# Linear attention on a megakernel's fourth layer: the share of EPS in every feature, from products of four rows to transfers and VectorE

## The chip, the core and the metric

The kernel runs on one core of one Trainium2 chip. A core has TensorE for matrix products (PE in the profile, with its weight loads as PEld), VectorE (DVE), ScalarE (ACT), GpSimd (POOL) and SyncE (SP), which issues the transfers. Every engine works through its own list of instructions in order; semaphores order the engines among each other. TensorE writes its results to PSUM, a small memory of eight banks, and the other engines read them there. Everything is in float32.

The metric is device time in microseconds for one launch that computes all four layers for both images of the batch. The kernel before takes 5482.62 us (median of three runs, 5473.6 to 5488.54).

## What is computed

The network has four attention or pooling layers on x of shape (2, 512, 64, 64), each on the group-normalised x and added to it. The change touches the fourth, a linear attention with positive random features (FAVOR), with 8 heads of 64 channels, 4096 tokens per image and m = 256 features:

```python
def _favor_softmax_features(data, proj, is_query):
    data_dash = jnp.einsum('bhnd,md->bhnm', data * normalizer, proj)
    diag = 0.5 * jnp.sum((data * normalizer) ** 2, axis=-1, keepdims=True)
    if is_query:
        stab = jnp.max(data_dash, axis=-1, keepdims=True)
    else:
        stab = jnp.max(data_dash, axis=(-2, -1), keepdims=True)
    return ratio * (jnp.exp(data_dash - diag - stab) + EPS)      # EPS = 1e-4
...
qp = _favor_softmax_features(q, proj, is_query=True)
kp = _favor_softmax_features(k, proj, is_query=False)
context = jnp.einsum('bhnm,bhnd->bhmd', kp, v)
k_sum = jnp.sum(kp, axis=-2)
denom = jnp.einsum('bhnm,bhm->bhn', qp, k_sum)
out = jnp.einsum('bhnm,bhmd->bhnd', qp, context) / denom[..., None]
out = out.transpose(0, 2, 1, 3).reshape(B, N, C) @ Wo
```

A query feature is exp(s - diag - stab) + EPS. Numerator and denominator of the attention may both be multiplied by exp(diag + stab) of their token and head. Then the features are plain exp(s), and EPS becomes one number per token and head, w = EPS * exp(diag + stab), which multiplies the sum of the context over all 256 features (in the numerator) and the sum of k_sum over all features (in the denominator). That is a product of one row of 512 tokens with one row of 64 channels for each head. How this addition is made is what the change is about.

## The kernel before

The kernel treats one image after the other, and the layers in turn. The fourth layer (`layer3`) has two parts. `key_context` goes over the tokens in eight blocks of 512 and gathers `ctxm` (features by heads and channels, with the part that EPS adds for the keys) and `ksum`; its end, `contexts`, overlaps with the first query block's preparation (`Queries.first`). `Queries.run` then goes over the same eight blocks for the queries. P is 128 partitions, TB = 512 tokens, KC = 4 chunks of 128 channels (two heads each), NK = 256 features, NB = 8 blocks.

Two generators make a query block. `Queries.prepare(blk + 1)` makes the queries of the next block: per chunk four products with the weights (through the helper at L133), a copy to `k` with the bias (L1330), squares on GpSimd (L1332), and the score products that serve only to find the largest score per token (L1363), whose maxima VectorE takes from PSUM (L1584). After the fourth chunk it sums the squares (L1341), transposes them (L1347), adds half the norm and the maximum (L1592, `losts`), takes the exponential into `wide` (L1596), in rows 32 c and 32 c + 1 of chunk c, and copies each pair of rows once more into the next chunk's stripe (L1597, L1598), so that four rows lie ready. A transpose (L1602) and a copy (L1604) turn this into `lost_rows`, with tokens along the free dimension.

`Queries.attend(blk)` uses the block that was prepared before. Per chunk it makes the features by products (L1664) and exponentials on ScalarE (L1667), and GpSimd forms `qf_sum`, both halves of the features weighted with `ksum` (L1617, L1619). One chunk later come the sums over features:

- L1631: four products of four rows with 64 columns, `ends` by `lost_rows`. They put the share of EPS into `psD` (denominator) and `psO` (numerator) of both heads. They lie in different stripes of rows and columns of TensorE's array.
- L1635: four products that add the features by `ctxm` to `psO`.
- L1639: two products that add `qf_sum` by `ksum` to `psD`.
- L1642 and L1643: VectorE takes the reciprocal of `psD` and multiplies `psO` with it; the result goes into the place of the queries, `k`.

After four chunks L1648 multiplies with the output weights (four output chunks of four products), L1651 adds the result to x, and L1652 sends it out. The two generators are woven into each other by `in_turn`, and the framework's planner then orders each engine's list by its own estimates, so that an instruction can stand earlier than in the source. `psD` has one PSUM buffer, `psO` two, and the general tile `mm` five.

`ends` is made once per image in `contexts` (L1498 to L1506): two sums over all features by products with ones, 512 wide, then eight small VectorE operations that scale them by 1e-4 and mask them, so that each of the four rows has its own head's values. `row2` is one of the masks, and comes from an input of its own.

Of the kernel before, what the change touches and what calls it, by code (L numbers as in the profile page):

```python
# [8 lines left out]
F32 = mybir.dt.float32  # L9
I32 = mybir.dt.int32  # L10
AF = mybir.ActivationFunctionType
ALU = mybir.AluOpType
# [3 lines left out]
P = 128  # L16
C = 512
KC = C // P
# [914 lines left out]
class Net(General):  # L933
# [353 lines left out]
    def layer3(self, X, Y, d, dst, after_keys):  # L1287

        tc, nc, vec = self.tc, self.nc, self.vec
        with tc.tile_pool(name="l3", bufs=1) as sp:
            proj = sp.tile([P, NK], F32, name="proj")
            nc.sync.dma_start(proj, d["proj"])
            nc.vector.tensor_scalar(proj, proj, HD ** -0.25, None, ALU.mult)

            e2h = sp.tile([P, 32], F32, name="e2h")
            nc.vector.memset(e2h, 0.0)  # L1300
            nc.vector.tensor_scalar(e2h[:, :2], self.e2, 0.5 * HD ** -0.5, None, ALU.mult)
            ctxm = sp.tile([P, 2, NH, HD], F32, name="ctxm")
            ksum = sp.tile([P, 2, NH], F32, name="ksum")

            ends = sp.tile([P, 2, P], F32, name="ends")
            with tc.tile_pool(name="l3b", bufs=2) as wp:
                queries = Queries(self, X, proj, e2h, ctxm, ksum, ends, wp)
                with tc.tile_pool(name="l3a", bufs=1) as kp, \
                        tc.tile_pool(name="l3p", bufs=8, space=PSUM) as pp:
                    row2 = kp.tile([P, P], F32, name="row2")  # L1310
                    nc.sync.dma_start(row2, d["row2"])
                    nmean, rstd, mv = self.group_stats(X, sp, pp, self.mv)
                    self.key_context(X, Y, d, nmean, rstd, mv, row2, queries, kp, wp, pp)
                if after_keys:
                    after_keys()
                with tc.tile_pool(name="l3f", bufs=1) as fp, \
                        tc.tile_pool(name="l3m", bufs=5, space=PSUM) as pp, \
                        tc.tile_pool(name="l3o", bufs=2, space=PSUM) as ppo, \
                        tc.tile_pool(name="l3d", bufs=1, space=PSUM) as ppd:
                    queries.run(dst, fp, pp, ppo, ppd, Y if after_keys else None)  # L1320
        self.ahead.close()
# [42 lines left out]
                                     proj[lo:lo + HD, :], start=True, stop=True)  # L1364
        return pS

    def key_context(self, X, Y, d, nmean, rstd, mv, row2, queries, kp, wp, pp):


        nc = self.nc  # L1370
# [81 lines left out]
        in_turn(prepare(0))  # L1452
        for blk in range(NB - 1):
            in_turn(contract(blk), prepare(blk + 1))
        in_turn(chain(contract(NB - 1), self.contexts(top, acc, asum, vmean, row2, queries, kp, pp)),
                queries.first(nmean, rstd, pp))

    def contexts(self, top, acc, asum, vmean, row2, queries, kp, pp):

        nc, ctxm, ksum = self.nc, queries.ctxm, queries.ksum  # L1460

# [31 lines left out]
            nc.vector.tensor_tensor(ksum[:, j, :], ps[:, :NH], lost, ALU.add)  # L1493
            yield
        ends = queries.ends
        for i, src in enumerate((ctxm, bcast(ksum, 3, HD))):
            ps = pp.tile([P, TB], F32, name="mm")
            for j in range(2):  # L1498
                nc.tensor.matmul(ps, self.one, src[:, j], start=(j == 0),
                                 stop=(j == 1))  # L1500
            for cc in range(KC):
                lo = 32 * cc if i else 32 * ((cc + 1) % KC)
                q = slice(lo, lo + 32)
                mine = self.cst[q, C_ROW:C_ROW + P] if i else row2[q, :]
                nc.vector.scalar_tensor_tensor(ends[q, i, :], ps[q, cc * P:(cc + 1) * P], 1e-4,
                                               mine, ALU.mult, ALU.mult)  # L1506
        yield


# [16 lines left out]
class Queries:  # L1526


    def __init__(self, net, X, proj, e2h, ctxm, ksum, ends, wp):
        self.net, self.nc, self.X, self.proj, self.e2h = net, net.nc, X, proj, e2h  # L1530
        self.ctxm, self.ksum, self.ends, self.wp = ctxm, ksum, ends, wp
        new = lambda shape, name: wp.tile(shape, F32, name=name, bufs=1)
        self.bq = new([P, KC], "bq3")
        self.tops, self.lost = (new([P, N // P, NH], name) for name in ("tops", "losts"))
        self.wide = new([P, NT, P], "wide")
        self.nc.gpsimd.memset(self.wide, 0.0)
        self.made = {}
# [35 lines left out]
    def prepare(self, blk, pp):  # L1573
# [18 lines left out]
        nc.vector.tensor_tensor(src, cols, tops[:, ts].rearrange("p t (c h) -> p t c h", h=2),  # L1592
                                ALU.add)

        w = wide.rearrange("p t (c r) -> p t c r", r=32)
        nc.scalar.activation(w[:, :, :, :2], src, AF.Exp)  # L1596
        nc.scalar.copy(w[:, :, 1:, 2:4], w[:, :, :3, :2])  # L1597
        nc.scalar.copy(w[:, :, 0, 2:4], w[:, :, 3, :2])  # L1598
        yield
        ps = pp.tile([P, TB], F32, name="mm")  # L1600
        for t in range(NT):
            nc.tensor.transpose(ps[:, t * P:(t + 1) * P], wide[:, t, :], net.ident)  # L1602
        rows = self.wp.tile([P, TB], F32, name="lost_rows")
        nc.scalar.copy(rows, ps)  # L1604
        self.made[blk] = qs, rows
        yield

    def attend(self, blk, ratio, dst, fp, pp, ppo, ppd):
        nc, X, ends, ctxm, ksum = self.nc, self.X, self.ends, self.ctxm, self.ksum
        qs, rows = self.made.pop(blk)  # L1610
        made_f, sums = {}, {}
        for i in range(KC + 1):
            if i < KC:
                made_f[i] = f = self.features(qs[:, i], fp, pp)
# [6 lines left out]
            if i:  # L1621
                cc = i - 1
                f = made_f.pop(cc)
                psD = ppd.tile([P, TB], F32, name="psD")
                psO = ppo.tile([P, TB], F32, name="psO")
                heads = [slice(h * HD, (h + 1) * HD) for h in range(2)]
                for ch in heads:
                    for i2, ps in ((1, psD), (0, psO)):

                        lo = 32 * cc if i2 else 32 * ((cc + 1) % KC)  # L1630
                        nc.tensor.matmul(ps[ch, :], ends[lo:lo + 4, i2, ch], rows[lo:lo + 4, :],  # L1631
                                         start=True, stop=False)
                for j in range(2):
                    for h, ch in enumerate(heads):
                        nc.tensor.matmul(psO[ch, :], ctxm[:, j, 2 * cc + h, :], f[h][j],  # L1635
                                         start=False, stop=(j == 1))
                for h, ch in enumerate(heads):
                    g = 2 * cc + h
                    nc.tensor.matmul(psD[ch, :], ksum[:, 0, g:g + 1].to_broadcast([P, HD]),  # L1639
                                     sums[cc][h], start=False, stop=True)  # L1640

                nc.vector.reciprocal(qs[:, cc, :], psD)  # L1642
                nc.vector.tensor_tensor(qs[:, cc, :], psO, qs[:, cc, :], ALU.mult)  # L1643
                yield
        for oc in range(KC):
            ps = pp.tile([P, TB], F32, name="mm")
# [693 lines left out]
def arrays_of(i):  # L2340
# [49 lines left out]
    for q in range(4):  # L2390
        for h in range(2):
# [12 lines left out]
        "taps": taps,  # L2404
        "tok32": np.pad(tok.reshape(P, KC, 2, 9).transpose(0, 1, 3, 2).reshape(P, KC, 18),
                        ((0, 0), (0, 0), (0, 14))),

        "row2": (p[:, None] % 32 == 2 + p[None, :] // HD).astype(f), "bv_row": b_kv[None, C:],
        "pb_rows": np.broadcast_to(a["L0_conv_b_proj"], (P, C)),
        "bproj_row": a["L0_conv_b_proj"][None, :],  # L2410
        "W_q": a["L0_conv_W_q"], "W_kv": a["L0_conv_W_kv"], "W_sr": a["L0_conv_W_sr"],
# [27 lines left out]
```

## Time and profile before

| | before |
|---|---|
| median time | 5482.62 us |
| span of the profiled run | 5487.7 us |
| TensorE (PE) busy | 5220.8 us, 95% |
| VectorE (DVE) busy | 3060.8 us, 56% |
| ScalarE (ACT) busy | 1797.6 us, 33% |
| GpSimd (POOL) busy | 1802.7 us, 33% |
| moved by DMA | 276.37 MB, 50 GB/s over the span |
| mean granted TensorE clock | 0.970 |
| L1631, products of four rows | 512 records, 587 to 741 ns each, median 638 |
| L1642, reciprocal | 64 times 3357 ns |
| L1643, product with the reciprocal | 64 times 687 ns |

The instructions of a line are listed with the engine, the tile written and the tiles read, the shape, the number, and the time of one. TensorE's records overlap, since its products are pipelined and products in different stripes of the array run side by side; what a group costs is read from the start of its first record to the start of the next group. A float32 product shows as two records. The query parts of the fourth layer lie at about 2295 to 2760 us (first image) and 5000 to 5480 us (second image).

### The profile page before, as it was taken

How to read it: one execution, taken by the hardware profiler on the slowest of the kernel's cores; microseconds unless marked ns; L12 is line 12 of the kernel's file. 1: busy time of each engine (PE TensorE's matmuls, PEld its weight loads, DVE VectorE, ACT ScalarE, POOL GpSimd, SP SyncE). 2: the span in 40 equal slices, each digit the busy share in tenths (PEclk: the TensorE clock that was granted, in tenths of full speed). 3: DMA queues.
4: the chain of work that ended last, by engine and by line, in shares of the span. 5: the costliest groups of instructions: out<-in, count | busy, mean ns of one | idle time of the engine just before them, and what ended most of it. 6: DMA issues, size and time to landing. Idle time of an engine off the chain costs nothing. (4 is left out here: it accounts for less than half of the span.)

```text
span 5487.7 us, 51928 instructions
## 1 busy us (share of the span) xinstructions
PE 5220.8 (95%) x19291; PEld 2262.9 (41%) x19291; DVE 3060.8 (56%) x3804; ACT 1797.6 (33%) x3441; POOL 1802.7 (33%) x1198
## 2 busy tenths in 40 slices
PE   7999999999988899999999999999999889999999
PEld 4433333554333444544344333335543334445443
DVE  3256667745679533544432666666456894334444
ACT  1245555233213233212212555542432222332221
POOL 0025555401310145434400355553013001554443
PEclk9999999999989999999999999999999999999999
DMA  3024445500000000200010344454000000000000
GB/s 140 2 66 118 126 125 157 148 18 24 1 2 0 1 1 3 75 21 34 31 53 2 83 126 126 125 150 148 1 24 1 2 0 1 1 8 16 16 16 24
DMA packets 103354, 276.37 MB, mean 50 GB/s; under 512 B 15090, under 2 KB 28146, under 8 KB 101044
## 3 DMA queue, kind: packets, MB, share of 16 engines
q1 hardware_dynamic: 103092, 272.97, 17.0%
q8 instruction: 154, 2.52, 0.2%
q14 instruction: 108, 0.88, 0.1%
HBM read 224.68 MB, written 48.23 MB: 50 GB/s over the span
## 5 line engine op out<-in xcount | busy, mean ns | idle before, releaser
L133 PE MATMUL mm<-big,w 128*128 128x512 f32 x2560 | 1186.4, 608 | 5.2 <-DVE late L2223 5.1
L133 PEld LDWEIGHTS mm<-big,w 128*128 128x128 f32 x2560 | 467.0, 191 | 685.1 <-issue 587.6
L2270 POOL TENSOR_TENSOR late<-late,big 128x1024 f32<-128x1024 f32 x192 | 454.5, 2367 | 302.2 <-DVE big L2266 292.3
L1265 POOL TENSOR_TENSOR total<-prob 128x512 f32<-128x512 f32 x128 | 159.6, 1269 | 759.6 <-ACT prob L1262 759.6
L1617 POOL TENSOR_SCALAR qf_sum<-qf,ksum_ratio 128x512 f32<-128x512 f32 x128 | 198.8, 1562 | 552.5 <-ACT qf L1667 351.6
L1182 PE MATMUL acc<-big,dg 128*128 128x512 f32 x704 | 318.9, 610 | 58.0 <-DVE big L697 27.1
L1438 POOL TENSOR_TENSOR big<-big 128x512 f32<-128x512 f32 x224 | 277.4, 1272 | 237.0 <-ACT big L1429 237.0
L2191 POOL TENSOR_TENSOR late<-late 128x512 f32<-128x512 f32 x128 | 160.6, 1275 | 490.5 <-ACT late L2180 448.3
L1642 DVE RECIPROCAL k<-psD 128x512 f32<-128x512 f32 x64 | 214.8, 3357 | 185.0 <-PE psD L1639 185.0
L697 DVE TENSOR_TENSOR big<-big 128x3968 f32<-128x3968 f32 x72 | 308.8, 4289 | 6.9 <-ACT big L698 0.5
L2266 DVE TENSOR_TENSOR big<-big,mm 128x512 f32<-128x512 f32 x384 | 254.4, 679 | 87.4 <-ACT mm L2263 85.9
L1429 ACT ACTIVATE big<-mm,ed 128x256 f32<-128x256 f32 x512 | 193.8, 489 | 277.8 <-DVE top L1425 250.1
L2263 ACT COPY mm<-big 128x512 f32<-128x512 f32 x384 | 220.5, 594 | 158.1 <-DMA big<-rows 117.8
L1363 PE MATMUL mm<-proj,k 64*128 64x256 f32 x2048 | 266.0, 392 | 0.9 <-ACT k L1330 0.9
L1282 DVE RECIPROCAL recip<-psD 128x512 f32<-128x512 f32 x64 | 214.9, 3357 | 87.2 <-PE psD L1279 87.2
L1262 ACT ACTIVATE prob<-mm 128x512 f32<-128x512 f32 x256 | 132.0, 605 | 364.4 <-PE mm L1259 359.2
L1584 DVE TENSOR_REDUCE tops<-mm 128x2 f32<-128x512 f32 x256 | 159.3, 680 | 163.5 <-PE mm L1363 163.3
L2131 DVE TENSOR_TENSOR prod<-qs,big 128x1024 f32<-128x1024 f32 x192 | 230.4, 1215 | 31.1 <-PE tap L2144 29.1
L2270 POOL TENSOR_TENSOR late<-late,tap 128x1024 f32<-128x1024 f32 x96 | 226.6, 2361 | 62.8 <-DVE tap L2266 44.3
L1363 PEld LDWEIGHTS mm<-proj,k 64*128 64x128 f32 x2048 | 208.1, 188 | 95.1 <-issue 78.7
L133 PE MATMUL mm<-big,big 128*128 128x512 f32 x512 | 239.7, 631 | 0.0
L2144 PE MATMUL tap<-prod,cst 128*32 128x512 f32 x768 | 228.7, 618 | 8.7 <-DVE prod L2131 8.6
(369 smaller groups left out, 8397.4 us busy)
## 6 DMA issues: line engine op xcount, KB each, us to landing
big<-rows SPq DMA_DIRECT2D x384, 256.0 KB, 4.0
tap<-rows SPq DMA_DIRECT2D x192, 256.0 KB, 4.0
yd<-late SPq DMA_DIRECT2D x32, 512.0 KB, 4.0
out<-big SPq DMA_DIRECT2D x64, 256.0 KB, 2.0
big<-in_W_kv SPq DMA_DIRECT2D x8, 1024.0 KB, 6.0
rows<-late SPq DMA_DIRECT2D x64, 128.0 KB, 2.4
big<-yd SPq DMA_DIRECT2D x16, 512.0 KB, 4.5
big<-in_x SPq DMA_DIRECT2D x4, 2048.0 KB, 7.6
```

What stands on the lines that cost most here:

```text
L133: self.nc.tensor.matmul(ps, w[:, kc, :], X[:, kc, blk * TB:(blk + 1) * TB], start=(kc == 0), stop=(kc == KC - 1))
L697: nc.vector.tensor_tensor(o, a, b, ALU.max)
L1182: nc.tensor.matmul(accs[b], dg, src[:, b * TB:(b + 1) * TB], start=(j == 0), stop=(j == 6))
L1282: nc.vector.reciprocal(r, psD)
L1363: nc.tensor.matmul(pS[h][i][:, t, :], k[lo:lo + HD, tok:tok + P], proj[lo:lo + HD, :], start=True, stop=True)
L1438: nc.gpsimd.tensor_tensor(a, a, part, ALU.add)
L1642: nc.vector.reciprocal(qs[:, cc, :], psD)
L2131: self.nc.vector.tensor_tensor(self.prods[k % 3].rearrange("p (y x) -> p y x", x=W), qs, self.kx[:, y + dy:y + dy + self.UY, dx:dx + W], A ...
L2144: nc.tensor.matmul(ps[32 * q:32 * q + 32, :], self.cst[:, C_TAPW + 16 - 2 * k:C_TAPW + 48 - 2 * k], self.prods[k % 3][:, j * TB:(j + 1) * ...
L2263: nc.scalar.copy(ps, part)
L2266: nc.vector.tensor_tensor(part.rearrange("p (y x) -> p y x", x=W), self.vx[:, y:y + self.UY // 2, dx:dx + W], ps.rearrange("p (y x) -> p y ...
L2270: nc.gpsimd.tensor_tensor(out, out, self.taps[k % 3], ALU.add)
```

## The change

The share of EPS no longer goes through TensorE. `prepare` writes the eight rows of `lost_rows` (four chunks, two heads) to a tile in DRAM with two transfers. In `attend`, `fetch` reads a head's row of 512 tokens back onto all 64 channels of that head: two transfers of 64 x 512 per chunk, into the tile `lost_all`, which has one buffer. `ends` becomes a column per chunk and kind, so that VectorE can use it as a value per partition. VectorE adds the share to `psD` in place, takes the reciprocal in place, adds the share to `psO` into `lost_all`, and multiplies the two. The fetch for the next chunk stands after that.

`ends` is now made by 32 products of one column instead of four of 512 columns; the masks, the input `row2` and the two copies of rows in `wide` go. `lost_rows` has one buffer instead of two.

```diff
@@ contexts
-        for i, src in enumerate((ctxm, bcast(ksum, 3, HD))):
-            ps = pp.tile([P, TB], F32, name="mm")
-            for j in range(2):
-                nc.tensor.matmul(ps, self.one, src[:, j], start=(j == 0),
-                                 stop=(j == 1))
-            for cc in range(KC):
...
-                nc.vector.scalar_tensor_tensor(ends[q, i, :], ps[q, cc * P:(cc + 1) * P], 1e-4,
-                                               mine, ALU.mult, ALU.mult)
+        ps = pp.tile([P, TB], F32, name="mm")
+        for i in range(2):
+            for g in range(NH):
+                ch = slice(g % 2 * HD, (g % 2 + 1) * HD)
+                for j in range(2):
+                    src = ksum[:, j, g:g + 1].to_broadcast([P, HD]) if i else ctxm[:, j, g, :]
+                    at = i * KC + g // 2
+                    nc.tensor.matmul(ps[ch, at:at + 1], src, self.one[:, :1], start=(j == 0),
+                                     stop=(j == 1))
+        nc.vector.tensor_scalar(ends, ps[:, :2 * KC].rearrange("p (i c) -> p i c", i=2), 1e-4,
+                                None, ALU.mult)
@@ Queries.prepare
-        nc.scalar.copy(w[:, :, 1:, 2:4], w[:, :, :3, :2])
-        nc.scalar.copy(w[:, :, 0, 2:4], w[:, :, 3, :2])
...
-        rows = self.wp.tile([P, TB], F32, name="lost_rows")
+        rows = self.wp.tile([P, TB], F32, name="lost_rows", bufs=1)
         nc.scalar.copy(rows, ps)
-        self.made[blk] = qs, rows
+        lost = self.yp.tile([2, KC, TB], F32, name="lost")
+        for h in range(2):
+            nc.sync.dma_start(lost[h], rows[h:P:32, :])
+        self.made[blk] = qs, lost
@@ Queries.attend
+        def fetch(cc):
+            ends_of[cc] = t = fp.tile([P, TB], F32, name="lost_all")
+            for h in range(2):
+                nc.sync.dma_start(t[h * HD:(h + 1) * HD, :], bcast(lost[h, cc], 0, HD))
+
+        fetch(0)
...
-                for ch in heads:
-                    for i2, ps in ((1, psD), (0, psO)):
-
-                        lo = 32 * cc if i2 else 32 * ((cc + 1) % KC)
-                        nc.tensor.matmul(ps[ch, :], ends[lo:lo + 4, i2, ch], rows[lo:lo + 4, :],
-                                         start=True, stop=False)
...
-                nc.vector.reciprocal(qs[:, cc, :], psD)
-                nc.vector.tensor_tensor(qs[:, cc, :], psO, qs[:, cc, :], ALU.mult)
+                t = ends_of.pop(cc)
+                nc.vector.scalar_tensor_tensor(psD, t, ends[:, 1, cc:cc + 1], psD, ALU.mult,
+                                               ALU.add)
+                nc.vector.reciprocal(psD, psD)
+                nc.vector.scalar_tensor_tensor(t, t, ends[:, 0, cc:cc + 1], psO, ALU.mult, ALU.add)
+
+                nc.vector.tensor_tensor(qs[:, cc, :], t, psD, ALU.mult)
+                if cc + 1 < KC:
+                    fetch(cc + 1)
```

## The prediction

> **What bounds the kernel now.** First the page, engines and slices:
>
> ```profile
> PE 5220.8 (95%) x19291; PEld 2262.9 (41%) x19291; DVE 3060.8 (56%) x3804; ACT 1797.6 (33%) x3441; POOL 1802.7 (33%) x1198
> ...
> L1642 DVE RECIPROCAL k<-psD 128x512 f32<-128x512 f32 x64 | 214.8, 3357 | 185.0 <-PE psD L1639 185.0
> ```
>
> TensorE is busy 95% of the span, VectorE 56%: time taken off TensorE counts unless a wait takes its place. The fourth layer runs once for each image. In its query part, about 2295 to 2760 and 5000 to 5480 us, one block of 512 tokens takes 61.3 us; the windows of two such blocks, one per image (columns: length, then busy us of PE, PEld, DVE, ACT, POOL, then clock, DMA share, GB/s):
>
> ```profile
> 2400.20:2461.50 61.30, 61.30 (x257) 26.33 (x256) 28.64 (x29) 12.72 (x25) 26.31 (x20) 1.00 0.05 18
> 5113.00:5174.30 61.30, 61.30 (x257) 26.32 (x256) 28.64 (x30) 12.73 (x25) 26.31 (x20) 1.00 0.05 18
> ```
>
> TensorE has no gap, at full clock; DVE and DMA are mostly idle. So TensorE sets the length of a block. Its timeline at the end of a block, start and length in the first two columns:
>
> ```profile
> 2441.94 0.64 PE L1631 MATMUL psD<-lost_rows,ends 4*64 4x512 f32 x1
> ...
> 2442.96 1.94 PE L1635 MATMUL psO<-qf,ctxm 128*64 128x512 f32 x8
> 2444.72 1.03 PE L1639 MATMUL psD<-qf_sum,ksum 128*64 128x512 f32 x4
> 2445.68 3.70 PE L133 MATMUL mm<-big,w 128*128 128x512 f32 x8
> 2449.32 0.64 PE L1631 MATMUL psO<-lost_rows,ends 4*64 4x512 f32 x1
> ...
> 2450.33 1.94 PE L1635 MATMUL psO<-qf,ctxm 128*64 128x512 f32 x8
> 2452.10 1.03 PE L1639 MATMUL psD<-qf_sum,ksum 128*64 128x512 f32 x4
> 2453.06 2.00 PE L1363 MATMUL mm<-proj,k 64*128 64x256 f32 x16
> 2454.99 3.89 PE L1648 MATMUL mm<-k,w 128*128 128x512 f32 x8
> 2458.80 1.07 PE L1341 MATMUL mm<-sq,e2h 128*32 128x512 f32 x8
> 2459.80 0.70 PE L1648 MATMUL mm<-k,w 128*128 128x512 f32 x1
> ```
>
> Read starts against starts. The four products of four rows (L1631) run beside each other and cost 2442.96 - 2441.94 = 1.02 us per channel chunk; all undisturbed ones of the 64 read 1.01 or 1.02. A block has four chunks, G0 to G3, whose L1631 start 11.3, 11.3, 7.4 and 31.3 us apart: the short gap is the one from G2 to G3. VectorE in it:
>
> ```profile
> 2445.83 3.36 DVE L1642 RECIPROCAL k<-psD 128x512 f32<-128x512 f32 x1 [2.45 <-PE psD L1639]
> 2449.22 0.69 DVE L1643 TENSOR_TENSOR k<-psO,k 128x512 f32<-128x512 f32 x1
> 2453.20 3.36 DVE L1642 RECIPROCAL k<-psD 128x512 f32<-128x512 f32 x1 [3.29 <-PE psD L1639]
> 2456.48 0.63 DVE L1584 TENSOR_REDUCE tops<-mm 128x2 f32<-128x512 f32 x1
> 2457.02 0.67 DVE L1643 TENSOR_TENSOR k<-psO,k 128x512 f32<-128x512 f32 x1
> ```
>
> After G3's L1639 ends (2453.06) VectorE needs until 2457.7, and the last L1648 of the first output chunk waits for it. By lengths TensorE needs 1.93 + 3.43 + 0.1 + 1.0 = 6.46 us up to the L1648 of 2459.80 and takes 6.74: 0.28 us of wait.
>
> **What the Trainium skill says.** (1) "TensorEngine Tiling (Array Packing)", Key Properties: a change of tiling mode drains TensorE. The trace agrees: eight L1648 take 3.43 us before products of the same tile shape and 3.53 before another, 0.1 us per switch. (2) "TensorE: Matmul & The Clock Gate", Part 1: The HAM clock gate: an idle window of about 3.4 us halves the clock. In the trace it takes less: an idle stretch of some 1.7 us (4408.9 to 4410.7) left the clock at 1.00, one of 2.7 (3668.5 to 3671.1) was followed by half clock. Windows of 1 us, PE busy is the second number, the clock the third from the right:
>
> ```profile
> 4409.00:4410.00 1.00, 0.00 (x0) 0.00 (x0) 1.00 (x1) 0.38 (x1) 0.00 (x0) 1.00 0.00 0
> ...
> 3670.00:3671.00 1.00, 0.00 (x0) 0.00 (x0) 1.00 (x1) 0.72 (x2) 0.97 (x1) 1.00 1.10 246
> ...
> 3673.00:3674.00 1.00, 1.00 (x3) 0.42 (x2) 1.00 (x2) 0.56 (x1) 0.46 (x1) 0.50 0.26 49
> ```
>
> Such an episode loses 1.7 us, summed over its windows. (3) "DMA: Bandwidth & Descriptors", Anatomy of one DMA, puts the fixed cost of one at about 2.0 us; the trace's smallest loads (64 KB) land after 1.9 to 2.0.
>
> **The change, part by part.** I call D the end of a chunk's L1639 (D2 for G2, D3 for G3).
>
> Removed on TensorE: L1631, 4 x 1.02 = 4.08 us per block. In the built order two of the eight score products (L1363 before) move between psO's and psD's products of G3, which adds two mode switches, 0.2. Net -3.9 us per block.
>
> Added on VectorE, per chunk: two scalar_tensor_tensor; reciprocal and product stay. The nearest rows are L553 (0.75, one PSUM operand) and L1643 (0.69); I take 0.70. The chain becomes 0.15 + 0.70 + 3.36 + 0.70 + 0.69 + 0.1 of hand-overs = D + 5.7 (before D + 4.2). psD has one buffer and is now held to the last of these. G0 to G1 and G1 to G2: the next L1639 starts 9.3 us after D (11.3 - 1.02 - 0.96), so it doesn't wait. G2 to G3: 3.64 (L133) + 1.77 (psO) + 0.5 + 0.1 = D2 + 6.0; GpSimd's sums, which L1639 also needs, are done at D2 + 5.8 already now (2451.49). So 0.3 us to spare. VectorE gets 4 x 1.4 = 5.8 us more per block, 34 of 57: no bound.
>
> Added transfers: two writes and eight reads of 128 KB per block. The first read of a block follows about 7 us after the copy of the rows (2407.1), and its chunk ends at 2423: hidden. The other three wait for the last VectorE operation on the single lost_all buffer, D + 5.7; the second transfer is issued 0.33 us later (the L1652 issue takes 332 ns). Time to land: nearest row is proj, 128 KB from DRAM, 2.5 us; floor 2.0, ceiling 4.0 (the row of 256 KB loads). I take 2.5: data at D + 5.75 + 0.33 + 2.5 + 0.1 = D + 8.7. The next chunk ends at D + 10.3 in the long gaps: hidden by 1.6. In the short one D3 = D2 + 6.95, so VectorE starts at D3 + 1.7. Queued behind it are G3's chain and one score reduction that is put into it, then another: 0.70 + 0.63 + 3.36 + 0.70 + 0.63 + 0.69 + 0.1 = 6.8, so k is ready at D3 + 8.5. In the built order TensorE has, before it needs k: six score products 1.5, three L1648 2.65, L1341 1.0, three L1648 of the next output chunk (these come earlier than before) 2.65, two transposes 0.3: D3 + 8.1. Wait 0.4 against 0.28 now: +0.1. Ends: 0 with a landing of 2.0, 1.9 with one of 4.0.
>
> So -3.8 us per ordinary block. There are seven per image; the first block of the first image is left out, since VectorE is full there (24 BATCH_NORM_STATS2 from 2286 on, G0 to G1 take 12.5): 13 x -3.8 = -49.
>
> ACT's two copies per block (0.2 each) and the row2 load go: off the path, nothing.
>
> Sums for `ends`, once per image: from the first L1499 (2278.88) to L1664 (2286.11) is 7.2 us now. It becomes 32 products of one column, 64 passes. L1491 has such at 128 weight columns: 3.65 us / 32 = 0.114 at full clock, 6.95 / 32 = 0.217 at half. With 64 columns I bound one by half of these and the whole; the clock is at half there (2269 to 2284), so 7 to 14, taken as 9.5 with the 0.9 of L1602: +3, and +1 for a clock that stays low longer. +4 x 2 = +8 (0 to 18).
>
> Last block of an image, no products of a next one: chunk after chunk is VectorE 5.6, transfer 2.8, so 8.4 apart, against 7.8, 7.3, 7.1 now; from G0's D (5.85 after its start, set by GpSimd): 0.15 + 5.6 + 3 x 8.4 = 31 for the last k, then four L1648 left, 3.4 at full clock, 6.9 at half: about 43.5 against 41.3 (5439.09 to 5480.36). +2.5 x 2 = +5 (0 to 12).
>
> Sum: -49 + 8 + 5 = -36: **5447 us**.
>
> **Rivals.** *The transfer takes the place of the products, in part*: landing 4.0. k comes 1.5 later, -2.3 per block, 13 x -2.3 = -30; three fetches each in the last blocks +9; +13 as above: -8, 5475. For it: the 256 KB loads read 4.0. Against: those run beside others, here DMA is 5% busy. *The wait halves the clock*: landing of 5 or so (64 reads of the same 2 KB in DRAM, which no row shows). The wait is then over 2.5 and draws 1.7 of half clock: -3.9 + 2.6 + 1.7 - 0.3 = +0.1 per block, last blocks +13 + 5, sums +8: about +27, **5510**, slower. Against: 0.05 DMA share. *Nothing is given back*: landing 2.0, sums at their floor, last blocks even: 13 x -4.1 = -53, 5430.
>
> **How the numbers follow.** Forecast 0.58, late transfer 0.16, halved clock 0.12, nothing given back 0.14. Faster by over 0.3% (below 5466) are forecast and floor, all but 0.01: 0.71; within: the late transfer, 0.17; slower: 0.12. The range 5424 to 5478 leaves out the halved clock and a little on either side.
>
> **What would show it.** Blocks 57.5 us apart with TensorE full and clock 1.00; lost_all landing in 2.3 to 2.8; VectorE's first operation of G3 waiting for a DMA, of G0 to G2 for psD; L1655 (the old L1648) waiting under 0.5 us for VectorE. Wrong, if the clock column falls to 0.5 once a block, if psD's product waits for VectorE in the short gap, or if the 64 one-column passes take over 14 us.

## The result, and the profile after

The changed kernel takes **5444.11 us** (median of four runs, 5439.77 to 5451.38) beside 5483.76 for the kernel before on the same chip: a ratio of 0.9931, 95% interval 0.9913 to 0.995. On another chip it was 5458.11 beside 5487.34, 0.9949 (0.9935 to 0.9963). It is faster, by a little over half a per cent.

The two pairs differ by ten microseconds, so single effects are not read from the total below but from stages of the profiled run. From the first product of `ends` to the end of an image the changed kernel took 466.5 and 463.3 us (images 0 and 1) on the first chip and 466.0 and 463.6 on the second. The stretch that no edit touches, from the end of image 0's queries to the first product of `ends` in image 1, took 2233.7 and 2251.1. The stages, in us, image 0 and image 1:

| stage | before | after |
|---|---|---|
| first product of `ends` to the end of G0's psD product, first block | 20.3, 20.6 | 20.3, 20.2 |
| from there to the same product of the last block (seven blocks) | 426.8, 425.6 | 406.8, 405.5 |
| from there to the end of the image | 37.6, 36.1 | 39.4, 37.6 |
| sum | 484.7, 482.3 | 466.5, 463.3 |

The sums fall by 18.2 and 19.0, 37.2 together; the span of the profiled run falls by 38.1 (5487.7 to 5449.6). The gain lies in the seven blocks, 20.0 each time; the last block gives back 1.8 and 1.5; the sums for `ends` cost nothing.

The lines of the page that answer to those shown of before (L1655 is the old L1648, the product with the output weights):

```profile
PE 5161.0 (95%) x18891; PEld 2254.2 (41%) x18891; DVE 3144.7 (58%) x3918; ACT 1793.0 (33%) x3409; POOL 1803.2 (33%) x1198
...
L1655 PE MATMUL mm<-k,w 128*128 128x512 f32 x512 | 242.0, 612 | 14.1 <-DVE k L1648 14.1
```

TensorE has 60 us less to do and VectorE 84 more. The second line is new in kind: TensorE now stands 14.1 us in front of this product, all of it until VectorE's last operation of a chunk (L1648) has written `k`: 8.7 us in the fourteen blocks before the last ones, the rest in front of the last products of the two images. The windows of two blocks of image 1 (length, then busy us of PE, PEld, DVE, ACT, POOL, clock, DMA share, GB/s):

```profile
5074.20:5132.10 57.90, 57.69 (x228) 25.43 (x226) 34.20 (x38) 12.45 (x24) 26.37 (x21) 1.00 0.11 37
5132.20:5190.20 58.00, 57.66 (x226) 25.41 (x226) 34.16 (x38) 12.41 (x24) 26.34 (x21) 1.00 0.10 37
```

A block takes 58 us, not 61.3, at full clock; before, PE's first number equalled the length, now 0.2 to 0.3 us are missing. Over the first six blocks of image 1 the mean is 58.3 (349.8 / 6; before 367.8 / 6 = 61.3). Where TensorE stands is in its timeline after G3's psD product (L1640), which ends at 5144.05, D3:

```profile
5142.34 0.70 PE L1362 MATMUL mm<-proj,k 64*128 64x256 f32 x4
5142.97 1.08 PE L1640 MATMUL psD<-qf_sum,ksum 128*64 128x512 f32 x4
...
5149.24 2.84 PE L1655 MATMUL mm<-k,w 128*128 128x512 f32 x6
5151.92 0.38 PE L1346 MATMUL mm<-cst,sq 128*128 128x128 f32 x2
5152.65 1.98 PE L1655 MATMUL mm<-k,w 128*128 128x512 f32 x4 [0.34 <-DVE k L1648]
```

The last product waits 0.34 us for `k`. In the seven blocks of image 1 this wait is 0.2 to 1.4 us, 4.38 together, 0.63 each. VectorE in the same stretch:

```profile
5144.71 1.29 DVE L1583 TENSOR_REDUCE tops<-mm 128x2 f32<-128x512 f32 x2 [2.20 <-PE mm L1362]
5146.20 0.76 DVE L1643 SCALAR_TENSOR_TENSOR psD<-lost_all,ends,psD 128x512 f32<-128x512 f32 x1 [0.20 <-DMA lost_all<-lost]
5146.86 0.69 DVE L1583 TENSOR_REDUCE tops<-mm 128x2 f32<-128x512 f32 x1
...
5151.91 0.68 DVE L1648 TENSOR_TENSOR k<-lost_all,psD 128x512 f32<-128x512 f32 x1
```

G3's first operation starts at D3 + 2.15, released by the transfer, and `k` is there at D3 + 8.54. This is one of the quicker blocks: in all seven of image 1 the fetch is issued at D3 - 1.5, but G3 starts between D3 + 2.0 and D3 + 3.2, and the wait for `k` is long where G3 starts late (0.21 us for a start at 2.02, 1.41 for one at 3.22). In the last block nothing covers the transfer. VectorE there:

```profile
5409.83 0.69 DVE L1648 TENSOR_TENSOR k<-lost_all,psD 128x512 f32<-128x512 f32 x1
5414.12 0.75 DVE L1643 SCALAR_TENSOR_TENSOR psD<-lost_all,ends,psD 128x512 f32<-128x512 f32 x1 [3.61 <-DMA lost_all<-lost]
```

From the end of one chunk's work to the start of the next it waits 3.6 us for the data, and so after each of the first three chunks (3.61, 3.74, 3.58). These two places, the short gap and the last block, are what the experiments take apart.

### The profile page after: what moved, and what is told of

Same layout as the page of the kernel before. It is cut to its first block, busy times and chain, and to the rows that moved or that the text cites. A ratio compares the mean times of both kernels' runs of the same rounds, so it can differ in the third digit from the quotient of the medians.

```text
span 5449.6 us, 51666 instructions
## 1 busy us (share of the span) xinstructions
PE 5161.0 (95%) x18891; PEld 2254.2 (41%) x18891; DVE 3144.7 (58%) x3918; ACT 1793.0 (33%) x3409; POOL 1803.2 (33%) x1198
## 5 line engine op out<-in xcount | busy, mean ns | idle before, releaser
L1362 PE MATMUL mm<-proj,k 64*128 64x256 f32 x2048 | 268.9, 393 | 0.9 <-ACT k L1329 0.9
L1655 PE MATMUL mm<-k,w 128*128 128x512 f32 x512 | 242.0, 612 | 14.1 <-DVE k L1648 14.1
L1583 DVE TENSOR_REDUCE tops<-mm 128x2 f32<-128x512 f32 x256 | 161.5, 684 | 160.2 <-PE mm L1362 159.9
L1362 PEld LDWEIGHTS mm<-proj,k 64*128 64x128 f32 x2048 | 206.5, 188 | 105.7 <-issue 90.1
```

What stands on the lines that cost most here:

```text
L1362: nc.tensor.matmul(pS[h][i][:, t, :], k[lo:lo + HD, tok:tok + P], proj[lo:lo + HD, :], start=True, stop=True)
L1655: nc.tensor.matmul(ps, self.wo[:, kc, oc * P:(oc + 1) * P], qs[:, kc, :], start=(kc == 0), stop=(kc == KC - 1))
```

## The experiments

The theory after the result: **the transfer**. `lost_all` has one buffer, so a fetch starts only when the chunk before is done, and in the short gap and in the last block its data comes late. The rival: **the chain**, four VectorE operations from psD to `k`, is too long wherever the data is. The first four runs set these against each other. Line numbers below are each kernel's own and shift by a few.

**Two buffers.** The fetches stand one chunk further ahead.

```diff
-        rows = self.wp.tile([P, TB], F32, name="lost_rows", bufs=1)
+        rows = sqs[1]
...
-            ends_of[cc] = t = fp.tile([P, TB], F32, name="lost_all")
+            ends_of[cc] = t = fp.tile([P, TB], F32, name="lost_all", bufs=2)
...
         fetch(0)
+        fetch(1)
...
-                if cc + 1 < KC:
-                    fetch(cc + 1)
+                if cc + 2 < KC:
+                    fetch(cc + 2)
```

> The changed kernel with two lost_all buffers, the first two chunks fetched at the start of a block and chunk cc+2 after chunk cc (lost_rows lies in a buffer of sqs, to make room). Transfer theory: what keeps a block at 58.0 us, not 57.3, is that the one lost_all buffer is fetched late, so that in the short gap VectorE starts G3 2.15 us after D3. With two buffers it starts at D3 + 0.15, k is ready near D3 + 6.7 to 7.0 in place of 8.5, the 0.4 to 1.8 us of wait at L1655 go, blocks are 57.3 to 57.6 us apart, and the gaps of 3.6 us between the chunks of the last blocks go (3 x 3 x 2 = 18 us at most, less what GpSimd and TensorE then bound): about 5425 us, 0.989 of before. Chain theory (rival): the four VectorE operations on the way from psD to k are the limit, wherever the data is: blocks stay at 58, last blocks at 41 to 42: 5440 to 5446, 0.993.

Measured: 5437.25 us, 0.990 (0.9885 to 0.9915). The last block is as the transfer theory has it: 31.8 us to the end of the image in both images, in place of 39.4 and 37.6. VectorE there:

```profile
5406.01 0.69 DVE L1649 TENSOR_TENSOR k<-lost_all,psD 128x512 f32<-128x512 f32 x1
5407.97 0.76 DVE L1644 SCALAR_TENSOR_TENSOR psD<-lost_all,ends,psD 128x512 f32<-128x512 f32 x1 [1.27 <-PE psD L1641]
```

The wait of 3.61 for the transfer has become one of 1.27 for psD. The ordinary blocks are a miss: 58.1 us, when 57.3 to 57.6 were expected. VectorE starts G3 at once, and TensorE waits all the same, for something else. First TensorE, then VectorE:

```profile
5146.58 4.56 PE L1656 MATMUL mm<-k,w 128*128 128x512 f32 x10 [0.67 <-DVE tops L1583]
```

```profile
5140.73 0.76 DVE L1644 SCALAR_TENSOR_TENSOR psD<-lost_all,ends,psD 128x512 f32<-128x512 f32 x1 [1.61 <-PE psD L1641]
5141.39 0.69 DVE L1583 TENSOR_REDUCE tops<-mm 128x2 f32<-128x512 f32 x1
5141.99 3.36 DVE L1646 RECIPROCAL psD<-psD 128x512 f32<-128x512 f32 x1
...
5145.85 0.68 DVE L1583 TENSOR_REDUCE tops<-mm 128x2 f32<-128x512 f32 x1
```

G3's scores fill four of the five `mm` buffers, and each comes free when its reduction (L1583) is done. The first output chunk takes the fifth and the squares' sum (L1340) the first that comes free. Early data moved G3's chain ahead of the reductions in VectorE's list: only one stands before the reciprocal, the second runs at 5145.85, and the second output chunk, whose turn comes at 5145.9 with the end of L1340, waits until 5146.58 for that buffer. A wait of 0.63 for `k` was traded for one of 0.67 for `tops`.

**The products left out, nothing in their place.** The share of EPS is missing from the query's numerator and denominator, so this is a bound, not a version.

```diff
-                for ch in heads:
-                    for i2, ps in ((1, psD), (0, psO)):
-
-                        lo = 32 * cc if i2 else 32 * ((cc + 1) % KC)
-                        nc.tensor.matmul(ps[ch, :], ends[lo:lo + 4, i2, ch], rows[lo:lo + 4, :],
-                                         start=True, stop=False)
...
```

> The kernel before without the four products of four rows (L1631) and with nothing in their place: what EPS adds to numerator and denominator is left out of the computation. Products theory: 1.02 us for each of 64 chunks is what the change can win, 65 us; blocks 57.2 us apart (-4.1), the last blocks -2 to -4 each: 5415 to 5425 us, 0.988. Rival, a wait takes their place: without the products TensorE reaches the first L1648 that needs k earlier, VectorE's chain does not move, and G3's k is then the limit: blocks 58 or more, 5435 or more, 0.992, near the changed kernel.

Measured: 5421.11, 0.9874 (0.9857 to 0.9891), within the forecast of the products theory. The query parts are 901.1 us, 65.9 below before, where 64 x 1.02 = 65 was counted. Blocks are 57.7, not 57.2: with the short gap a microsecond shorter, G3's psD product reaches the end of GpSimd's sums. In TensorE's timeline it takes 1.54, not 1.03:

```profile
5122.66 1.54 PE L1633 MATMUL psD<-qf_sum,ksum 128*64 128x512 f32 x4
```

In the changed kernel two score products (four records, L1362 at 5142.34 above) stand in between, and that wait does not show.

**Four transfers in place of two**, the same bytes.

```diff
-                nc.sync.dma_start(t[h * HD:(h + 1) * HD, :], bcast(lost[h, cc], 0, HD))
+                for q in (slice(0, TB // 2), slice(TB // 2, TB)):
+                    nc.sync.dma_start(t[h * HD:(h + 1) * HD, q], bcast(lost[h, cc, q], 0, HD))
```

> The changed kernel with each fetch in four transfers of 64x256 in place of two of 64x512: the same bytes, two more issues on SyncE, 0.48 us each by the trace of the changed kernel, so the data comes about 1 us later. Transfer theory (a fetch after the previous chunk's last VectorE operation is on the path in the short gap and in the last blocks, and nowhere else): +1.0 per block x 14 and +1.0 x 3 in each of two last blocks = +20, about 5464 us, 0.996; more, 5475 to 5490, if the longer wait at L1655 halves the clock. Chain theory (rival): the transfer is hidden, 5440 to 5448.

Measured: 5460.72, 0.9943 (0.9928 to 0.9958), which overlaps with both measurements of the changed kernel. The stages show two effects that cancel. The last block is longer by 3.4 and 4.9 us, where 3 was expected. The ordinary blocks are shorter, 57.8 in place of 58.3, although the data is later: a miss for the transfer theory. VectorE in image 1:

```profile
5150.59 1.89 DVE L1583 TENSOR_REDUCE tops<-mm 128x2 f32<-128x512 f32 x3 [1.89 <-PE mm L1362]
5153.52 0.76 DVE L1644 SCALAR_TENSOR_TENSOR psD<-lost_all,ends,psD 128x512 f32<-128x512 f32 x1 [1.04 <-DMA lost_all<-lost]
```

D3 is 5149.93, so G3 starts at D3 + 3.6. But the planner, which orders by its own estimates, put three reductions ahead of it and TensorE's products with `k` later: all four transposes and one product of the third output chunk now come first. In image 0 that hides the late data altogether. In the fourth block (D3 is 2505.37) G3 starts at D3 + 3.0 and `k` comes at D3 + 9.0, and TensorE runs through without a wait:

```profile
2508.35 0.76 DVE L1644 SCALAR_TENSOR_TENSOR psD<-lost_all,ends,psD 128x512 f32<-128x512 f32 x1 [0.42 <-DMA lost_all<-lost]
...
2513.68 5.32 PE L1656 MATMUL mm<-k,w 128*128 128x512 f32 x12
```

From the second block to the sixth of image 0 the blocks are 57.4 to 57.7 us, and in the changed kernel 57.9 to 59.1. So in the ordinary blocks the order counts as much as the arrival, and TensorE's own order is part of it.

**The numerator first**, with two buffers, so that three operations and not four follow psD.

```diff
+                nc.vector.scalar_tensor_tensor(qs[:, cc, :], t, ends[:, 0, cc:cc + 1], psO, ALU.mult,
+                                               ALU.add)
                 nc.vector.scalar_tensor_tensor(psD, t, ends[:, 1, cc:cc + 1], psD, ALU.mult,
                                                ALU.add)
                 nc.vector.reciprocal(psD, psD)
-                nc.vector.scalar_tensor_tensor(t, t, ends[:, 0, cc:cc + 1], psO, ALU.mult, ALU.add)
-
-                nc.vector.tensor_tensor(qs[:, cc, :], t, psD, ALU.mult)
+                nc.vector.tensor_tensor(qs[:, cc, :], qs[:, cc, :], psD, ALU.mult)
```

> The kernel of two lost_all buffers, and the numerator's addition goes first and into qs, before psD is ready: three operations stay between psD and k (4.9 us by the trace's lengths, not 5.6). Transfer theory: the data was the limit, so after two buffers this brings little more: 1 to 3 us, 5422 to 5424. Chain theory: the length of the chain after D is the limit, so this brings its 0.7 us per block where two buffers alone brought nothing: 14 x 0.7 + 8 x 0.7 = 15, near 5428. Either way blocks are not below 57.2, the length without the products.

Measured: 5448.82, 0.9926 (0.9912 to 0.994). Both theories miss. The chain is shorter (the last blocks take 30.6 and 30.8, 1.0 and 1.2 less than with two buffers), and ordinary blocks are longer, 58.5. The planner put G3's psD product ahead of all scores again, where it takes 1.53, and the products that need `k` early, before the squares' sum. So neither arrival nor length of the chain alone decides an ordinary block.

**A new theory: the order.** After D3 VectorE has about 8 us of work that TensorE waits for: G3's chain, which ends in `k`, and the reductions, which free `mm`. Without waits, TensorE's own work lasts as long. So late data costs (`k` late), and an order with the reductions behind the chain costs as well (`tops` late); as long as TensorE asks for `k` as early as in the changed kernel, one must repair both to gain. Two lines make the other order: a step in the generator, so that the reductions are recorded before G3's reciprocal.

**Two buffers and the reductions first.** Against the kernel with two buffers:

```diff
+                if cc == KC - 1:
+                    yield
                 nc.vector.reciprocal(psD, psD)
```

> The kernel of two lost_all buffers, with one more step of the generator between the first and the second VectorE operation of chunk G3. In the built order two of the score reductions (L1583) then stand ahead of G3's reciprocal, and the other two ahead of k, where in the kernel of two buffers one stands ahead of the reciprocal, one ahead of k and two behind it. Order theory: in the kernel of two buffers the transfer is out of the way, and what is left is that TensorE's second output chunk waits 0.67 us per block for the second reduction, which frees a PSUM buffer of mm, because that reduction stands behind the chain. Freed at D3 + 2.1 here, the wait goes; k comes near D3 + 8.2, and TensorE needs it at D3 + 8.2. Blocks 57.4 to 57.7, not 58.1, last blocks as with two buffers: 14 x 0.5 = 7 us less than that kernel, 5428 to 5432 where it had 5437. Rival (VectorE's list is full after D3, so every order costs TensorE about 0.7): the wait moves to k, blocks stay at 58.0 to 58.2 and the time at 5437.

Measured: 5423.74, 0.9885 (0.9867 to 0.9902), and in a second measurement 5423.93, 0.9882 (0.986 to 0.9904). Blocks are 57.2 us, even less than the 57.4 to 57.7 expected. A window of one:

```profile
5071.20:5128.40 57.20, 57.20 (x228) 25.51 (x226) 34.18 (x38) 12.41 (x23) 26.34 (x20) 1.00 0.11 38
```

PE's time equals the length again. The products of the output weights now run through in TensorE's timeline; D3 is 5127.78, and `k` comes at 5135.65, before the first product that needs it:

```profile
5133.31 4.46 PE L1658 MATMUL mm<-k,w 128*128 128x512 f32 x10
```

The step changed TensorE's list too: the squares' sum (L1340) now stands ahead of all products of the output weights, and the transposes ahead of the second output chunk. What this brings and what the place of the reductions brings is not separated. The order alone, below, has the same order on TensorE in this stretch; it differs from this kernel only by the buffers and the place of `lost_rows`.

The same kernel again:

> The kernel with two buffers and the reductions first once more, beside the other two: blocks 57.2 us apart with no wait of TensorE in them, query parts of 451 us from the first product of ends to the image's end, 0.987 to 0.990 of before.

**The order alone**, with one buffer and the late fetch: the changed kernel plus the same two lines.

> The changed kernel, one lost_all buffer and the late fetch, with the extra step of the generator for G3 alone. In the built order two reductions stand ahead of G3's first VectorE operation, two between it and the reciprocal. Both-theory (in the blocks either thing alone is worth little, since a late chain and a late reduction each cost TensorE about 0.7): the data comes near D3 + 2.0 as in the changed kernel, so k is ready near 2.15 + 0.76 + 1.3 + 3.4 + 0.67 + 0.2 + 0.7 = D3 + 9.1, and TensorE needs it at D3 + 8.2: a wait of 0.8 to 0.9 us, blocks near 58.0, last blocks 37.5 to 39 as in the changed kernel, total 5450 to 5458, 0.994. Order theory alone (the order is the whole loss in the blocks, and the transfer is hidden there): blocks 57.2 to 57.4, last blocks 37.5 to 39: 12 us above the kernel with two buffers and this order, 5436, 0.991.

Measured: 5452.28, 0.9933 (0.9915 to 0.995), blocks 58.3, last block 37.7 in image 1: no better than the changed kernel, as the both-theory says. TensorE in the same place (D3 is 5144.51):

```profile
5153.27 1.98 PE L1657 MATMUL mm<-k,w 128*128 128x512 f32 x4 [0.48 <-DVE k L1650]
```

With the reductions ahead, `k` is late by the transfer. The four cases side by side, with the other kernels below: the mean of the first six blocks of image 1, the wait per block that TensorE's timeline names in the seven blocks of image 1, the last block of image 1, and both query parts together.

| | block | wait per block | last block | query parts |
|---|---|---|---|---|
| changed kernel | 58.3 | 0.63, for k | 37.6 | 929.8 |
| two buffers | 58.1 | 0.67, for tops | 31.8 | 914.4 |
| order alone | 58.3 | 0.79, for k | 37.7 | 930.6 |
| two buffers and order | 57.2 | 0 | 31.8 | 902.3 |
| before | 61.3 | (none named) | 36.1 | 967.0 |
| products left out | 57.7 | for GpSimd, inside psD's product | 29.3 | 901.1 |
| four transfers | 57.8 | 0.2, for k | 42.5 | 930.8 |
| numerator first | 58.5 | 0.67, for k | 30.8 | 916.1 |

In the ordinary blocks either repair alone brings 0.0 to 0.2 us and both together 1.1. In the last block the buffers bring it all. The four transfers show that this pair of repairs is not the only way: with one buffer and later data their blocks are shorter by 0.5 than the changed kernel's, because TensorE asks for `k` later.

**The placing of lost_rows alone**, control of the two buffers.

```diff
-        rows = self.wp.tile([P, TB], F32, name="lost_rows", bufs=1)
+        rows = sqs[1]
```

> The changed kernel with nothing but lost_rows placed in a buffer of sqs: the control of the kernel with two buffers, which needed that room. If the placing costs nothing, it does what the changed kernel does: blocks 57.8 to 58.5, last blocks with 9.1 to 9.3 us from chunk to chunk, 5444. If the placing were the reason of what two buffers brought, its last blocks would be 6 to 7 us shorter.

Measured: 5460.92, 0.9947 (0.9931 to 0.9964); blocks 58.3, last block of image 1 37.6. The placing costs and brings nothing that can be seen there. (In image 0 the last block took 41.2, where the changed kernel took 39.4 and 38.5; it is no shorter in either image.) Beside it the changed kernel once more:

> The changed kernel once more, beside the others on one chip: 0.993 of before (0.991 to 0.995), blocks 57.8 to 58.5 us apart, with the waits for k of 0.3 to 1.8 us per block at L1655 not the same in every block.

Measured as given under the result, 0.9949; waits for `k` of 0.3 to 1.3 us in the seven blocks of image 1, 4.49 together.

**The order in the kernel before**, control of the added step.

```diff
+                if cc == KC - 1:
+                    yield
                 nc.vector.reciprocal(qs[:, cc, :], psD)
```

> The kernel before, with its products of four rows, and the extra step of the generator ahead of G3's reciprocal: the control of what the step does by itself. If it is worth something only together with the moved addition, the kernel before has at most its 0.3 us of wait per block to win (61.3 to 61.0 at best, 4 us in all), or loses up to 0.8 per block if k now comes behind all four reductions: 5478 to 5495, 0.999 to 1.002. If the step shortened any version by its 1 us per block, as it does the kernel with two buffers, blocks would be 60.3 apart and the time 5472, 0.997.

Measured: 5498.4, 1.0012 (1.0003 to 1.0022); blocks 62.1, longer by 0.8. In the kernel before all four reductions stand behind G3's reciprocal already, one of them ahead of `k`. The step puts all four ahead of `k`, and in TensorE's list it moves the squares' sum (L1341) ahead of the output weights. The sum takes the fifth buffer, and the first output chunk waits for the first reduction:

```profile
5185.72 1.07 PE L1341 MATMUL mm<-sq,e2h 128*32 128x512 f32 x8
5187.89 3.70 PE L1650 MATMUL mm<-k,w 128*128 128x512 f32 x8 [1.11 <-DVE tops L1584]
```

```profile
5187.21 2.42 DVE L1584 TENSOR_REDUCE tops<-mm 128x2 f32<-128x512 f32 x4
```

So the step is no gain by itself; what counts is where it leaves the reductions and TensorE's own products.

**Twice the one-column passes** for `ends`.

```diff
-                for j in range(2):
-                    src = ksum[:, j, g:g + 1].to_broadcast([P, HD]) if i else ctxm[:, j, g, :]
+                for j in range(4):
+                    src = ksum[:, j % 2, g:g + 1].to_broadcast([P, HD]) if i else ctxm[:, j % 2, g, :]
...
-                    nc.tensor.matmul(ps[ch, at:at + 1], src, self.one[:, :1], start=(j == 0),
-                                     stop=(j == 1))
+                    nc.tensor.matmul(ps[ch, at:at + 1], src, self.one[:, :1], start=(j % 2 == 0),
+                                     stop=(j % 2 == 1))
```

> The changed kernel with each of the 64 one-column passes of ends made twice (the second time into the same place). My forecast priced one pass at 0.15 us, the trace of the changed kernel shows 32 in 1.7 to 1.9 us, 0.054 each at half clock. At 0.054 the 64 more cost 3.5 us per image from the first L1502 to G0's sums, or less where GpSimd's qf_sum sets their time; at 0.15, 9.5. If one-column products also keep the clock low, the half-clock stretch around them (22 us in the changed kernel, 15 before) grows by another 3 to 7 us.

Measured, in one run: from the first product of `ends` to the end of G0's psD product 24.4 and 24.7 us in place of 20.3 and 20.2, so 4.2 and 4.5 more for 64 passes, 0.07 each. The half-clock stretch, summed over windows of 1 us as in the prediction, loses 11.95 us in place of 10.24. That is near the lower price, and it rules out 0.15. The starts of the single passes say more. In the changed kernel they come in pairs, 27 and 80 ns apart by turns, 107 ns for a pair. In this run the first four and the last four of an image come singly, some 107 ns apart. So 107 ns is the price of one such pass by itself at half clock, and 0.054 comes from two that run side by side. The kernel gives neighbouring heads different halves of the array's columns, which is the likely reason; the trace does not name the halves.

**The numerator first in the last block only**, on top of two buffers and the order.

```diff
+                last, d = blk == NB - 1, qs[:, cc, :]
+                if last:
+                    nc.vector.scalar_tensor_tensor(d, t, ends[:, 0, cc:cc + 1], psO, ALU.mult,
+                                                   ALU.add)
...
-                nc.vector.tensor_tensor(qs[:, cc, :], t, psD, ALU.mult)
+                nc.vector.tensor_tensor(d, d if last else t, psD, ALU.mult)
```

> The kernel with two buffers and the reductions first, and in the last block of an image, where no scores are made, the numerator's addition goes first and into qs. Theory: without products of a next block the four VectorE operations after D follow one another, so the chunk spacing there is the chain's length wherever GpSimd does not set it; the kernel with the numerator first had 30.6 to 30.8 us for that stretch in place of 31.8. So -1.1 per image, 2 us in all: blocks stay at 57.2, 5420 to 5423. Rival (GpSimd's sums set the spacing there): no change, 5423 to 5425.

Measured: 5417.84, 0.9865 (0.9843 to 0.9886), the fastest of all by its median, though the interval overlaps with that of the kernel without it. The stage carries it: the last block takes 30.6 in both images, 1.2 to 1.3 less, and the blocks stay at 57.2. Both query parts together take 897.5 us, 69.5 below before. That is 3.7 less than with the products left out, since that kernel's blocks, at 57.7, still wait for GpSimd's sums.

## Why the prediction was right

The total was right: 5447 forecast, 5444 measured, and so was the mechanism: the products' time comes off TensorE, and the late transfer gives a part of it back in the short gap and in the last block. That the total came within 3 us is luck: the terms missed by 11.5 us in one direction and by 13.7 in the other.

- **The products, -4.08 per block.** Right. Without waits a block is 57.2 (two buffers and order), 4.1 below before. Read from start to start over six blocks, L1631 takes off 4.07. The score products that now stand between psO's and psD's product cost 0.35, not 0.2, since a switch shows behind it as well as before it: of the records of 128 x 128 products in the kernel before, the last one ahead of a switch takes 0.52 us and the first one behind it 0.53, the others 0.43. The products of the output weights take 0.34 less, the wait of before (0.28) among it, so the two nearly cancel.
- **The wait in the short gap, 0.4, so -3.8 per ordinary block.** The mechanism was right to the operation: G3's first operation waits for the DMA (in the block shown D3 + 2.15, forecast D3 + 1.7), `k` comes at D3 + 8.54 (forecast 8.5: the later data and a list of VectorE that is 0.4 shorter than counted cancel), and L1655 waits for it. Over the seven blocks of image 1 `k` comes at D3 + 8.4 to 9.6, 8.8 in the mean. The size was off: 0.63 us named by the waits, and 58.3 - 57.2 = 1.1 in all against the blocks without any. The waits named count from the modelled end of the record before, so they say too little. From start to start 0.81 of the 1.1 lies at the transposes and the wait behind them (0.44 to 1.25 us per block), and 0.26 in the products of the output weights, which stand in another order. The thirteen ordinary blocks brought -37.5 (the seven of each image 40.1 in all, less 2.6 for the first of image 0), not -49: 11 us short.
- **The transfer.** The issue was wrong. SyncE's two issues take 1.08 us (5142.54 to 5143.62 in its timeline), 0.44 and 0.60, where 0.33 was counted for the second. The 0.33 was read from a store that is issued by itself. The kernel before had the right price among its other loads: at L2240 an issue takes 445 ns by itself and 590 directly behind another (medians). The landing of 2.5 holds in the last block, where 3.6 us from the last VectorE operation to the data leave 2.5 behind the issues; in the blocks it is the quick end: G3 starts 2.4 to 3.6 us behind the second issue. The floor was read a little wide of the page of before: 1.9 and 2.0 are its shortest landings, but not those of its smallest loads (26.5 KB took 7.8).
- **psD in the short gap, 0.3 to spare.** Held: in the seven blocks of image 1 L1640 never waits for VectorE; it waits once for GpSimd (1.81 us, at the first chunk of the last block, 1.04 before). In the first block of image 0, where VectorE is full, it waits for VectorE once, 1.31 us.
- **The first block of image 0, left out.** It saves 2.6 us (59.9 after 62.5), so it should have been counted.
- **The sums for `ends`, +8.** Wrong: 0.0 and -0.5. One pass is 0.054 us (32 within 1.73, from the first record to the next kind) and not 0.15. The lower bound, half of what 128 columns take, is right for a pass by itself (0.107, half of 0.213); that two passes can run side by side was left out. The 64 passes take 3.5 us where the products of 512 columns took 5.5 (2279.09 to 2284.61). What did come as forecast is a clock that stays low longer, 22 windows, not 15, which loses 10.24 us and not 6.83. The one works against the other, and the stage came out even.
- **The last block, +5.** Measured 1.8 + 1.5 = 3.3 by the stages; chunks are 9.1 to 9.3 us apart, not 8.4, since the issues are longer, and the last `k` of image 1 comes 33.1 us behind G0's D (5404.95), not 31. What made up for it is the clock: the four products of the output weights that are left run at full clock in 3.7 us (5438.09 to 5441.79), where the forecast's 43.5 holds only near its half-clock figure of 6.9.

So the thirteen blocks fell short by 11.5 us, and 8.5 in the sums for `ends`, 1.7 in the last blocks, 2.6 in the first block and 0.9 outside these stages came on top: -36 + 11.5 - 8.5 - 1.7 - 2.6 - 0.9 is the measured -38.

The rivals are settled too. The clock stayed at 1.00 in the ordinary blocks, so the halved clock fell. It did fall to 0.50 once in the last block of image 1, for some 3 us behind a wait of 2.85; but the kernel before has such a stretch in its last block too (5458 to 5461), and there TensorE had stood idle for no more than 0.57 us at a time in the ten microseconds before. So the length of one idle stretch, from which the forecast read the rule, does not alone decide when the clock falls; what does is open. The late transfer came true in part, by the issue everywhere and by the landing in some blocks. "Nothing is given back", 5430, is not what the changed kernel does; the kernels with two buffers and the order reach and pass it: 5424 and 5418.

## What to carry to other kernels

When work leaves the bound engine, look at the stretch where that engine next needs the helper's result, and list everything that the helper does there in its order: two kinds of results that the bound engine waits for share one list, and a repair of one can merely move the wait to the other. Look at the bound engine's own list too: work put ahead of the product that needs the result hides a late result (the four transfers in image 0). A buffer more was worth something here where nothing else covers the transfer (the last block), and inside the full loop only together with an order that suits it. And read effects of a few microseconds from stages: a part of this program that no edit touches took 17 us more in one run of the changed kernel than in another.

## What was not expected of the hardware

- Products of one column with 64 weight columns come at 0.054 us per pass at half clock. By itself such a pass takes 0.107, half of the 0.213 that the 128-column ones of the kernel before took at half clock; two of them can run side by side in that time.
- An issue on SyncE directly behind another takes longer than one by itself: 596 and 445 ns for the fetch (medians of 62 and 66), 590 and 445 for the loads at L2240 of the kernel before. The store of x that the forecast was read from took 332 by itself.
- A fetch of two such transfers has its data in place 3.6 us after the instruction that it waits for, where nothing else is in the way. In the ordinary blocks the same fetch, issued at the same place, lands at D3 + 2.15 in one block of image 1 and at D3 + 3.2 in another. Why it does is open.
